# Two score additions moved from VectorE into TensorE's transposed bank, and two list rounds cut to one half of the candidates, in a sparse GATv2 + GCN kernel

## The chip, the cores and the metric

One core of one Trainium2 chip. The metric is the device time of one execution in microseconds. Fourteen runs of the kernel before gave a median of 3408.0 us, from 3378.63 to 3419.2 us.

## The reference

The input is `x` (3327 x 128) and a sparse symmetric matrix `adj` (3327 x 3327) with weights between 0.05 and 1 on its edges and on its diagonal; a row has 63 neighbours off the diagonal on average. Two layers follow each other. The first is a graph attention of four heads on `h = relu(layernorm(x))`:

```python
x1 = x @ w1; x2 = x @ w2
E = leaky_relu(x1[:, None, :] + x2[None, :, :], 0.01)
s = tanh((E @ a) / 8) * 8
s = exp(s) * A_shape
s = s / sum(s, axis=-1)
out = leaky_relu(s @ x @ Wlin.T, 0.01)
```

The heads are joined, multiplied by `w` and added to `x`. The second layer is `x + relu(A_norm @ (layernorm_relu(x) @ W.T + b))`, where `A_norm` is `adj + I`, scaled on both sides by the inverse square root of its row sums.

## The kernel before, in words

The kernel pads to 3328 rows: 26 blocks of 128 rows. It does not compute the attention scores of all pairs. For each row it finds the columns with an edge and gathers only those.

**Preparing a block** is the generator `prep(b, k)`. It transposes the block of `adj` (L365) and stores it (L370), multiplies the parts that the second layer can already use (L379), marks the edges as codes (L410), and takes the largest eight codes of each of 64 column segments (L422) into `cand`, two halves of 136 candidates. `select(r)` then runs 13 rounds: a MAX8 over the candidates (L453) and, in all but the last, a MATCH_REPLACE8 that strikes those eight out (L456). Rounds 0 to 3 alternate between the two halves (136 wide); the later ones run over both (272 wide). The first 64 entries of the list become the indices `idx` of 32 gathered tiles; up to 40 more go to a shared overflow of 256 places for each 64 rows. A row or half-block that does not fit raises a flag, and the kernel then computes everything again in a dense form. Near its end `prep` computes `x1b` and `x1n` and the table `pex`: the own-row score term of the block, `pmx` (L561), is multiplied by `modsel` on TensorE (L566) and copied out of PSUM by ScalarE (L568).

**The main loop** runs over (block, half of 64 rows, group of four tiles). Eight tiles are a window: four windows `w` and one overflow window (`ge`, three tiles) for each half, ten windows for each block, 260 in all. GpSimd gathers the tiles (L595) into one of four buffers `g`. `stage_z` transposes the gathered features into the PSUM bank pair `z` (L622, two bank pairs in turn, `hp` 0 and 1), and VectorE takes the maximum with `x1n` into `r` (L638), one of 1024 columns for each bank pair. `stage_r` multiplies `r` by the attention vector (L657) into `s` once for two groups.

`finish(k, hb, w)` is a generator too, one for each window. ScalarE copies `s` to `ssb` (L666); TensorE transposes that four times into a PSUM bank `tr` (L675); VectorE adds the gathered score term of the neighbour (L678) and then `pex`, or for the overflow window a term of `ex` (L681), into `sc`; ScalarE applies tanh (L686) and exp (L688); VectorE multiplies by the edge weights to `wt` (L697); TensorE sums the rows into `ag` (L706, or L724 for the overflow window), and `allow` gives the gather buffer free. `close` finishes a half block (L735 to L797).

**The order** is written by hand. `slot()` is called at fixed places in `stage_z` and after `stage_r`, 108 times for each block, and moves each open `close`, then each open `finish`, on by one `yield`, then `prep`, then the gathers. So the number of `yield`s between two steps sets how many slots lie between them in every engine's queue. The engines run their queues in order. The banks `tr` come from a pool of two that `prep`, `finish` and `close` share.

Of the kernel before, what the change touches and what calls it, by code (L numbers as in the profile page):

```python
# [9 lines left out]
F32 = mybir.dt.float32  # L10
AF = mybir.ActivationFunctionType
OP = mybir.AluOpType
# [3 lines left out]
P = 128  # L16
SLOPE = 0.01
CAP = 8.0
# [44 lines left out]
OVT = 3  # L63
# [168 lines left out]
def _sparse_layers(tc, nc, x, adj, w1, w2, a, wlin, w, gw, gb, gb_sb, gwT, x_sb, dinv, flag, ident, out):  # L232
# [13 lines left out]
    NP, D = x.shape  # L246
    H = w1.shape[0]
# [5 lines left out]
    WT = 8  # L253
    NW = NT // WT
    LATE = 1

    with ExitStack() as l0:
# [19 lines left out]
        modsel = res.tile([P, P], F32, name="modsel")  # L277
# [8 lines left out]
        pb = l0.enter_context(tc.tile_pool(name="pb", bufs=2))  # L286
# [41 lines left out]
        def bank():  # L328
            return ps_tr.tile([P, 4, P], F32, name="tr").rearrange("p a b -> p (a b)")
# [23 lines left out]
        def prep(b, k):  # L353
# [41 lines left out]
            SOME = 8 + 4 * 32  # L395
            cand = pb.tile([P, 2, SOME + 4 * 32], F32, name="cand", bufs=1)
# [51 lines left out]
            flat = cand[:, :, :SOME]  # L448

            def select(r):  # L450
                top = lists[:, 8 * r:8 * r + 8]
                of = cand[:, r % 2, :SOME] if r < 4 else flat
                nc.vector.max(top, of)  # L453
                yield
                if 8 * r + 8 < 2 * SLOTS + EXTRA:
                    nc.vector.match_replace(out=of, in_to_replace=top, in_values=of, imm_value=0.0)  # L456
                yield

            for r in range(SLOTS // 4):
                yield from select(r)  # L460
# [7 lines left out]
            pm = bank()  # L468
# [8 lines left out]
            for r in range(SLOTS // 4, SLOTS // 4 + EXTRA // 8):  # L477
                yield from select(r)
# [17 lines left out]
            pm = bank()  # L496
# [22 lines left out]
            pm = bank()  # L519
            ex_ps = pm[:, :2 * OVT * 46].rearrange("p (t c) -> p t c", c=46)  # L520
            for c in range(2):
                for t in range(FOUND):
                    nc.tensor.matmul(ex_ps[:, OVT * c + t, :], oi[:, (FOUND * c + t) * P:(FOUND * c + t + 1) * P], ext[:, :46],
                                     start=True, stop=True)
# [25 lines left out]
            pm = bank()  # L550
            nc.tensor.matmul(pm, hTb, w1_sb.rearrange("p h d -> p (h d)"), start=True, stop=True)
            x1b = pb.tile([P, H * D], F32, name="x1b")
            nc.scalar.copy(x1b, pm)
            yield
            pm = bank()
            for h in range(H):
                nc.tensor.matmul(pm[:, h * P:(h + 1) * P], w1_sb[:, h, :], hTb, start=True, stop=True)
            x1n = pb.tile([P, H, P], F32, name="x1n")
            nc.scalar.activation(x1n, pm[:, :H * P].rearrange("p (h i) -> p h i", h=H), AF.Copy, scale=-1.0)
            pmx = pb.tile([P, 16, H], F32, name="pmx", bufs=1)  # L560
            nc.vector.tensor_tensor(pmx, tmask[:, :, None].to_broadcast([P, 16, H]),  # L561
                                    p_all[:, b, None, :H].to_broadcast([P, 16, H]), OP.mult)
            yield
            yield
            pm = bank()
            nc.tensor.matmul(pm[:, :16 * H], modsel, pmx.rearrange("p t h -> p (t h)"), start=True, stop=True)  # L566
            pex = pb.tile([P, 16, H], F32, name="pex")
            nc.scalar.copy(pex, pm[:, :16 * H].rearrange("p (t h) -> p t h", h=H))  # L568
            k.x1b, k.x1n, k.pex = x1b, x1n, pex
            yield  # L570

        def rows_in():
# [88 lines left out]
        def finish(k, hb, w):  # L661
            g, s = k.g.pop((hb, w)), k.s
            f0 = k.f0[hb]
            nt, nk, nm = (WT, 4, 2) if w < NW else (OVT, OVT, 1)
            ssb = ph.tile([P, BANK], F32, name="ssb", bufs=1)
            nc.scalar.copy(ssb[:, :nk * P], s[:, :nk * P])  # L666
            if w < NW:
                wq = pb.tile([P, WT, 8], F32, name="wq")
                diag = bass.AP(g.tensor, g.offset + BODY * hb, [list(g.ap[0]), [WIDE + 8, 8], [1, 8]])
                nc.vector.tensor_tensor(wq, diag, qmask[:, None, :].to_broadcast([P, WT, 8]), OP.mult)  # L670
            yield
            yield
            pt = ps_tr.tile([P, 4, P], F32, name="tr")
            for q in range(nk):
                nc.tensor.transpose(pt[:, q, :], ssb[:, q * P:(q + 1) * P], ident)  # L675
            yield
            sc = pb.tile([P, WT, H], F32, name="sc")
            nc.vector.tensor_tensor(sc[:, :nt].rearrange("p (m k) h -> p m k h", m=nm),  # L678
                                    pt.rearrange("p k (h m) -> p m k h", m=32)[:, :nm, :nk],
                                    g[:, :, f0 + D:f0 + D + H].rearrange("p (m k) h -> p m k h", m=nm), OP.add)  # L680
            nc.vector.tensor_add(sc[:, :nt], sc[:, :nt], k.pex[:, 8 * hb:8 * hb + 8] if w < NW else  # L681
                                 k.ex[:, OVT * hb:OVT * hb + OVT, 42:42 + H])
            yield
            yield
            th = pb.tile([P, WT, H], F32, name="th")
            nc.scalar.activation(th[:, :nt], sc[:, :nt], AF.Tanh, scale=1.0 / CAP)  # L686
            pe = pb.tile([P, WT, H], F32, name="pe")
            nc.scalar.activation(pe[:, :nt], th[:, :nt], AF.Exp, scale=CAP)  # L688
            yield
            yield  # L690

            if w == 0:
                k.ag = ps_a.tile([P, 2, 256], F32, name="ag")
            ag = k.ag
            if w < NW:
                wt = pv.tile([P, WT, H, 8], F32, name="wt", bufs=2)
                nc.vector.tensor_tensor(wt, pe[:, :, :, None].to_broadcast([P, WT, H, 8]),  # L697
                                        wq[:, :, None, :].to_broadcast([P, WT, H, 8]), OP.mult)
                yield
                yield  # L700
                yield
                yield
                yield
                for t in range(WT):
                    u, cg = t // 4, t % 4
                    nc.tensor.matmul(ag[32 * cg:32 * cg + 32, u, :WORK], wt[:, t].rearrange("p h q -> p (h q)"),  # L706
                                     g[:, t, f0:f0 + WORK], start=(w == 0 and t < 4), stop=False, skip_group_check=True)
                allow("g")
                return
            am = pb.tile([P, OVT, HALF], F32, name="am", bufs=1)  # L710
            wo = pv.tile([P, OVT, 8, H, 8], F32, name="wo")
            for t in range(OVT):
                nc.vector.scalar_tensor_tensor(am[:, t, :], code[:, :HALF], k.ex[:, OVT * hb + t, 41:42], g[:, t, BODY * hb:BODY * hb + HALF],
                                               op0=OP.is_equal, op1=OP.mult)
                nc.vector.tensor_tensor(wo[:, t], pe[:, t, None, :, None].to_broadcast([P, 8, H, 8]),
                                        am[:, t].rearrange("p (g q) -> p g q", q=8)[:, :, None, :].to_broadcast([P, 8, H, 8]), OP.mult)
                yield
            yield
            yield
            yield  # L720
            yield
            for t in range(OVT):
                for u in range(2):
                    nc.tensor.matmul(ag[:, u, :WORK], wo[:, t, 4 * u:4 * u + 4].rearrange("p g h q -> p (g h q)"),  # L724
                                     g[:, t, f0:f0 + WORK], start=False, stop=(t == OVT - 1), skip_group_check=True)
            allow("ge")
            tails.append(close(k, hb))
# [75 lines left out]
        for b in range(NB):  # L803
            k = Blk()
# [6 lines left out]
        SLOTP = 6 * 2 * NG  # L811
        AHEAD = 0.5
        preps = [prep(b, blks[b]) for b in range(NB)]
        queue = deque()
        done = [0] * NB
# [29 lines left out]
        def allow(kind):  # L845
            state[kind] += 1
# [345 lines left out]
        with tc.manual_schedule():  # L1192
# [5 lines left out]
            def scores(i):  # L1198
                if 0 <= i < n:
                    b, hb, m = groups[i]  # L1200
                    stage_r(blks[b], hb, m, rs.pop(i))
                    if m % 2 or m == NG - 1:
                        ends.append(finish(blks[b], hb, m // 2))
                    slot()

            for i in range(-1, n + 1):
                if i + 1 < n:
                    slot()
                if 0 <= i < n:
                    b, hb, m = groups[i]  # L1210
# [153 lines left out]
```

## Time and profile before

| | before |
|---|---|
| median of 14 runs | 3408.0 us |
| profiled execution, its own time | 3427.39 us |
| span in its trace | 3425.7 us |
| mean granted TensorE clock | 0.883 |
| TensorE busy | 2644.0 us (77%) |
| VectorE busy | 2102.3 us (61%) |
| GpSimd busy | 1713.6 us (50%) |
| ScalarE busy | 683.1 us (20%) |
| DMA | 241 GB/s on average |

The profiled execution is 0.6% slower than the median of the runs. Busy times of engines overlap, so they do not add up to the span. In the groups of instructions a row names a line, an engine, an operation, output and inputs, the count, the total and mean time, and what the engine had waited for. A TensorE record is one pass: a transposing product of 128 columns is one record, a plain 32-bit product two.

### The profile page before, as it was taken

The page shows a single profiled execution, that of the slowest core. Times are in us where ns is not written, and L with a number is a line of the kernel's source. Part 1 is how long each engine was busy: PE and PEld are TensorE (multiplying, and loading weights), DVE is VectorE, ACT ScalarE, POOL GpSimd, SP SyncE. Part 2 cuts the span into 40 slices and gives each one's busy share as a digit, 9 for nine tenths or more (in the row PEclk, how much of TensorE's full clock was granted, in tenths as well). Part 3 has the DMA queues.
Part 4 walks back from the last instruction along what each step waited for, and adds up shares of the span by engine and source line. Part 5 has one row for each costly group of instructions (what it writes and reads, how often), then busy time and mean ns, then how long its engine had stood idle before and what let it go on. Part 6 is the DMA issues. An engine that isn't in the chain of part 4 may idle for free.

```text
span 3425.7 us, 52385 instructions
## 1 busy us (share of the span) xinstructions
PE 2644.0 (77%) x19410; PEld 1847.8 (54%) x19410; DVE 2102.3 (61%) x6426; ACT 683.1 (20%) x1703; POOL 1713.6 (50%) x1822
## 2 busy tenths in 40 slices
PE   6687777777777777777877777777877787777887
PEld 4455555545555555555655555555655555555553
DVE  6676566657656666665665665665665665665442
ACT  3122122212212212221221121221221221221110
POOL 3555555455555555545545545455555555445530
PEclk8799889898989989888888888888888888888999
DMA  9978678678768867867867867767776777777886
GB/s 324 316 259 263 211 247 267 204 244 279 226 221 261 261 213 246 263 206 244 259 197 246 267 199 243 253 215 233 249 231 215 247 232 226 232 224 216 261 272 184
DMA packets 417844, 826.94 MB, mean 241 GB/s; under 512 B 38435, under 2 KB 288815, under 8 KB 414255
## 3 DMA queue, kind: packets, MB, share of 16 engines
q0 software_dynamic: 141440, 619.41, 55.8%
q1 hardware_dynamic: 165343, 147.87, 13.9%
q10 hardware_dynamic: 110800, 56.25, 5.6%
q8 instruction: 156, 2.56, 0.3%
q14 instruction: 105, 0.86, 0.1%
HBM read 754.47 MB, written 113.22 MB: 253 GB/s over the span
## 4 chain that ended last, share of the span: by engine, by line
PE 53%; DVE 17%; another core or an unknown queue 11%; issue 10%; DMA 4%; ACT 1%; POOL 1%; ACTq 0%; SPq 0%; DVEq 0%; POOLq 0%
PE z L622 19%; PE s L657 11%; DVE r L638 9%; PE ag L706 5%; PE z L627 3%; PE tr L675 3%; DVE cand L422 3%; PE ag L724 2%; PE tr L379 2%; DVE codes L410 1%; POOL g L595 1%; PE tr L757 1%; DMA g<-AT_d 1%; PE z L988 1%
## 5 line engine op out<-in xcount | busy, mean ns | idle before, releaser
L595 POOL DMA_INDIRECT g<-table,idx x1664 | 1591.9, 957 | 1386.1 <-PE ag L706 813.3
L638 DVE TENSOR_TENSOR r<-z,x1n 128x1024 f32<-128x1024 f32 x832 | 1013.3, 1218 | 849.1 <-remote 318.9
L622 PE MATMUL z<-ident,g 128*128 128x128 f32 x6656 | 1050.8, 302 | 169.5 <-issue 111.8
L622 PEld LDWEIGHTS z<-ident,g 128*128 128x128 f32 x6656 | 856.3, 157 | 354.7 <-issue 232.4
L657 PE MATMUL s<-r,sel 128*2 128x512 f32 (+1 forms) x3744 | 549.8, 610 | 128.5 <-DVE r L638 94.5
L706 PE MATMUL ag<-g,wt 128*32 128x133 f32 x3328 | 237.8, 306 | 103.2 <-issue 102.2
L666 ACT COPY ssb<-s 128x512 f32<-128x512 f32 x260 | 146.9, 565 | 831.0 <-PE s L657 331.5
L657 PEld LDWEIGHTS s<-r,sel 128*2 128x2 f32 x3744 | 82.3, 84 | 402.9 <-issue 259.3
L706 PEld LDWEIGHTS ag<-g,wt 128*32 128x32 f32 x3328 | 135.6, 118 | 225.3 <-issue 217.4
L675 PE MATMUL tr<-ident,ssb 128*128 128x128 f32 x988 | 172.4, 300 | 92.3 <-issue 74.4
L422 DVE MAX8 cand<-codes 128x8 f32<-128x52 uint16 x1664 | 217.4, 205 | 0.0
L675 PEld LDWEIGHTS tr<-ident,ssb 128*128 128x128 f32 x988 | 129.8, 155 | 117.7 <-issue 89.9
L379 PE MATMUL tr<-at,x_sb 128*128 128x128 f32 x488 | 100.1, 363 | 115.4 <-ACT at L367 112.5
L595 POOL DMA_INDIRECT ge<-table,idxo x104 | 98.5, 947 | 177.4 <-PE ag L724 93.4
L367 ACT COPY at<-tr 128x512 f32<-128x512 f32 (+1 forms) x175 | 97.3, 556 | 417.7 <-remote 223.1
L686 ACT ACTIVATE th<-sc 128x32 f32<-128x32 f32 x260 | 58.4, 225 | 534.2 <-DVE sc L681 294.0
L379 PEld LDWEIGHTS tr<-at,x_sb 128*128 128x128 f32 x488 | 84.5, 258 | 143.9 <-ACT at L367 135.8
L365 PE MATMUL tr<-ident,adjb 128*128 128x128 f32 x676 | 124.6, 311 | 33.1 <-DMA adjb<-in_adj_dram 15.3
L633 DVE TENSOR_TENSOR r<-z,x1n 128x128 f32<-128x128 f32 x104 | 30.2, 290 | 190.5 <-PE z L627 135.3
L627 PE MATMUL z<-oi,x1b 128*128 128x256 f32 x416 | 133.5, 405 | 3.2 <-issue 3.2
L453 DVE MAX8 lists<-cand 128x8 f32<-128x272 f32 (+1 forms) x338 | 133.3, 394 | 2.2
L622 PE MATMUL z<-ident,ge 128*128 128x128 f32 x416 | 87.5, 287 | 43.7 <-issue 35.7
(199 smaller groups left out, 2627.9 us busy)
## 6 DMA issues: line engine op xcount, KB each, us to landing
adjb<-in_adj_dram SPq DMA_DIRECT2D x26, 1664.0 KB
table<-AT_d SPq DMA_DIRECT2D x26, 1664.0 KB
AT_d<-at ACTq DMA_DIRECT2D x150, 256.0 KB
g<-table,idx POOLq DMA_INDIRECT x1664
table<-img SPq DMA_DIRECT2D x12, 1296.0 KB
adjb<-AT_d SPq DMA_DIRECT2D x72, 128.0 KB
g<-AT_d SPq DMA_DIRECT2D x25, 256.0 KB
g<-AT_d ACTq DMA_DIRECT2D x25, 256.0 KB
```

Source lines behind the costliest of these rows:

```text
L365: nc.tensor.transpose(pt[:, q, :], adjb[:, (j0 + q) * P:(j0 + q + 1) * P], ident)
L379: nc.tensor.matmul(pq[:, :P], x_sb[:, j0 + q, :], at[:, q, :], start=(q == 0), stop=(q == js[-1]))
L422: nc.vector.max(cand[:, c, 8:].rearrange("p (r s) -> p r s", s=32)[:, :, sgm % 32], codes.rearrange("p a b -> p (a b)")[:, sgm % 32 * SEG: ...
L453: nc.vector.max(top, of)
L595: return nc.gpsimd.indirect_dma_start(out=g[:, t, lo:hi], out_offset=None, in_=tab, in_offset=bass.IndirectOffsetOnAxis(ap=at[:, t:t + 1], ...
L622: nc.tensor.matmul(z[:, i, q * P:(q + 1) * P], g[:, m % 2 * 4 + q, c0:c0 + D], ident, is_transpose=True, start=(q == 0 or m < 8), stop=(m ...
L627: nc.tensor.matmul(z[:, i, :n], k.x1b[:, h * D:(h + 1) * D], k.oi[:, hb * n:(hb + 1) * n], start=False, stop=True, skip_group_check=True)
L638: nc.vector.tensor_tensor(r.rearrange("p h (i s) -> p h i s", s=16), z.rearrange("p h (i s) -> p h i s", s=16), k.x1n[:, 2 * hp:2 * hp + 2 ...
L657: nc.tensor.matmul(k.s[32 * h:32 * h + 2, :n], sel[:, h, 31 - at:33 - at], r[h // 2][:, h % 2, :n], start=(at == 0), stop=(at == 1 or m == 8))
L666: nc.scalar.copy(ssb[:, :nk * P], s[:, :nk * P])
L675: nc.tensor.transpose(pt[:, q, :], ssb[:, q * P:(q + 1) * P], ident)
L706: nc.tensor.matmul(ag[32 * cg:32 * cg + 32, u, :WORK], wt[:, t].rearrange("p h q -> p (h q)"), g[:, t, f0:f0 + WORK], start=(w == 0 and t ...
```

## The change

`select` keeps to one half of the candidates for six rounds instead of four. The table `pex`, its product, its copy and two `yield`s go; `pmx` is kept in two buffers and handed to `finish`. In `finish` the two VectorE additions and two `yield`s go. In their place TensorE adds two products of 32 columns (12 in the overflow window) to the bank in which the transposed scores lie: the neighbour's term times the identity, and `pmx` times `modsel` (or the `ex` term times the identity). Tanh reads the bank.

```diff
@@ in prep: select @@
-                of = cand[:, r % 2, :SOME] if r < 4 else flat
+                of = cand[:, r % 2, :SOME] if r < 6 else flat
@@ at the end of prep @@
-            pmx = pb.tile([P, 16, H], F32, name="pmx", bufs=1)
+            pmx = pb.tile([P, 16, H], F32, name="pmx")
             nc.vector.tensor_tensor(pmx, tmask[:, :, None].to_broadcast([P, 16, H]),
                                     p_all[:, b, None, :H].to_broadcast([P, 16, H]), OP.mult)
-            yield
-            yield
-            pm = bank()
-            nc.tensor.matmul(pm[:, :16 * H], modsel, pmx.rearrange("p t h -> p (t h)"), start=True, stop=True)
-            pex = pb.tile([P, 16, H], F32, name="pex")
-            nc.scalar.copy(pex, pm[:, :16 * H].rearrange("p (t h) -> p t h", h=H))
-            k.x1b, k.x1n, k.pex = x1b, x1n, pex
+            k.x1b, k.x1n, k.pmx = x1b, x1n, pmx
             yield
@@ in finish @@
             yield
             pt = ps_tr.tile([P, 4, P], F32, name="tr")
             for q in range(nk):
-                nc.tensor.transpose(pt[:, q, :], ssb[:, q * P:(q + 1) * P], ident)
-            yield
-            sc = pb.tile([P, WT, H], F32, name="sc")
-            nc.vector.tensor_tensor(sc[:, :nt].rearrange("p (m k) h -> p m k h", m=nm),
-                                    pt.rearrange("p k (h m) -> p m k h", m=32)[:, :nm, :nk],
-                                    g[:, :, f0 + D:f0 + D + H].rearrange("p (m k) h -> p m k h", m=nm), OP.add)
-            nc.vector.tensor_add(sc[:, :nt], sc[:, :nt], k.pex[:, 8 * hb:8 * hb + 8] if w < NW else
-                                 k.ex[:, OVT * hb:OVT * hb + OVT, 42:42 + H])
-            yield
+                nc.tensor.matmul(pt[:, q, :], ssb[:, q * P:(q + 1) * P], ident, is_transpose=True, start=(q == 0), stop=False,
+                                 skip_group_check=True)
+            sc = pt.rearrange("p k (h m) -> p m k h", m=32)[:, :nm, :nk]
+            parts = [(ident, g[:, :nt, f0 + D:f0 + D + H])]
+            if w < NW:
+                parts.append((modsel, k.pmx[:, 8 * hb:8 * hb + 8]))
+            else:
+                parts.append((ident, k.ex[:, OVT * hb:OVT * hb + OVT, 42:42 + H]))
+            for at, (by, term) in enumerate(parts):
+                nc.tensor.matmul(sc, by, term.rearrange("p (m k) h -> p m k h", m=nm), start=False, stop=(at == 1), skip_group_check=True)
             yield
             th = pb.tile([P, WT, H], F32, name="th")
-            nc.scalar.activation(th[:, :nt], sc[:, :nt], AF.Tanh, scale=1.0 / CAP)
+            nc.scalar.activation(th[:, :nt].rearrange("p (m k) h -> p m k h", m=nm), sc, AF.Tanh, scale=1.0 / CAP)
```

## Prediction

> **What bounds the kernel now.** I read the page first, its busy times and its chain of work.
>
> ```profile
> PE 2644.0 (77%) x19410; PEld 1847.8 (54%) x19410; DVE 2102.3 (61%) x6426; ACT 683.1 (20%) x1703; POOL 1713.6 (50%) x1822
> ...
> PE 53%; DVE 17%; another core or an unknown queue 11%; issue 10%; DMA 4%; ACT 1%; POOL 1%; ACTq 0%; SPq 0%; DVEq 0%; POOLq 0%
> PE z L622 19%; PE s L657 11%; DVE r L638 9%; PE ag L706 5%; PE z L627 3%; PE tr L675 3%; DVE cand L422 3%; PE ag L724 2%; PE tr L379 2%; DVE codes L410 1%; POOL g L595 1%; PE tr L757 1%; DMA g<-AT_d 1%; PE z L988 1%
> ```
>
> TensorE is the busiest engine and holds over half of the chain, but it idles for 23% of the span. VectorE holds a sixth. The two take turns: TensorE fills a `z` bank pair, VectorE reduces it to `r`, TensorE needs `r`. So what moving work from one to the other is worth depends on who waits for whom where the work sits. Then the waits:
>
> ```profile
> ACT th L686 <- DVE sc L681: 294.0, 102, 9.6
> ...
> DVE r L638 <- PE z L622: 269.7, 153, 5.2
> ```
>
> The columns are microseconds in total, times, longest. ScalarE waits for the additions, and VectorE waits for TensorE before `r`. ScalarE is 20% busy, so its wait costs only where TensorE waits for ScalarE in turn.
>
> The place of the change is just behind the four transposes L675. The timeline of one window, VectorE's lines first and then TensorE's (start, length, operation; in brackets the idle time before it):
>
> ```profile
> 1794.32 1.22 DVE L638 TENSOR_TENSOR r<-z,x1n 128x1024 f32<-128x1024 f32 x1
> 1795.45 0.19 DVE L678 TENSOR_TENSOR sc<-tr,g 128x32 f32<-128x32 f32 x1
> 1795.67 0.20 DVE L681 TENSOR_TENSOR sc<-sc,pex 128x32 f32<-128x32 f32 x1
> 1795.79 1.01 DVE L422 MAX8 cand<-codes 128x8 f32<-128x52 uint16 x8
> 1796.83 0.29 DVE L425 MAX8 cand<-cand 128x8 f32<-128x128 f32 x1
> 1797.04 1.21 DVE L638 TENSOR_TENSOR r<-z,x1n 128x1024 f32<-128x1024 f32 x1
> ...
> 1798.30 1.09 PE L622 MATMUL z<-ident,g 128*128 128x128 f32 x8 [1.62 <-issue]
> ```
>
> VectorE runs without a gap from `r` through the additions and the list work to the next `r`; TensorE has stood still for 1.62 us when that `r` ends at 1798.25. Here VectorE is the bound. In other windows it is the other way round, as this line shows: VectorE idles 2.56 us until TensorE has filled the bank.
>
> ```profile
> 1376.40 1.23 DVE L638 TENSOR_TENSOR r<-z,x1n 128x1024 f32<-128x1024 f32 x1 [2.56 <-PE z L627]
> ```
>
> I counted in the trace, for every window, whether the two products `r` that follow the additions on VectorE started at once behind other VectorE work or after more than 0.1 us of idling. Both at once: 103 windows. Both waited: 71. The first at once, the second waited: 63. The reverse: 21. (Two have no such pair.) It repeats by the place of a window in its block: the windows in which the code scan and the list rounds run are VectorE's, those in which `close`, `oi`, `x1b` and the overflow window run are TensorE's. Between the transposes and the next scores L657 TensorE's idle time has a median of 2.0 us in the 103, of 0.0 in the 71, of 0.2 in the 63 and of 2.8 in the 21.
>
> **The change, part by part**, against the profiled execution's 3427.4 us.
>
> *TensorE gains two plain 32-column products for each window*, four records with a 128-column weight each. Nothing in the trace has that shape, so its price comes from the nearest plain ones:
>
> ```profile
> 1754.81 0.43 PE L566 MATMUL tr<-pmx,modsel 128*128 128x64 f32 x2
> 1755.08 0.39 PE L622 MATMUL z<-ident,ge 128*128 128x128 f32 x2
> ```
>
> From the start of the two 64-column records to the next start it is 0.27 us at full clock. Start to start, the 16-column records of L470 and the 46-column ones of L523 and L525 have a median of 0.111 us at full and of 0.213 us at half clock; a 128-column transposing record takes 0.109. So up to 128 columns the width hardly matters. The mean granted clock of 0.883 means half clock for 23% of the time: 0.77 x 0.111 + 0.23 x 0.213 = 0.135 us a record, 0.54 us a window, 140 us in 260 windows if all of it lay on the path. Bounds: 0.44 us (all full clock) and 0.85 us (all half).
>
> The Trainium skill ("TensorE: Matmul & The Clock Gate", section "Back-to-back issue gap") gives matmuls of 1 to 64 columns a floor of about 25 ns instead. The 111 ns of L470 contradict it for a stream that loads new weights each time. By the page the sum below would be an estimate of some 65 us less, which is a gain.
>
> *TensorE loses* 26 products L566, two records each: 26 x 0.27 = 7 us, in the overflow-window part of a block, where TensorE is the bound. ScalarE's 26 copies L568 (0.22 us each) go too; ScalarE idles there: nothing.
>
> *VectorE loses the additions and part of four list operations a block:*
>
> ```profile
> L678 DVE TENSOR_TENSOR sc<-tr,g 128x32 f32<-128x32 f32 x208 | 38.7, 186 | 57.1 <-remote 31.1 <-PE tr L675 13.9 <-PE ag L724 2.9
> L681 DVE TENSOR_TENSOR sc<-sc,pex 128x32 f32<-128x32 f32 x208 | 40.0, 192 | 7.2
> ...
> L453 DVE MAX8 lists<-cand 128x8 f32<-128x272 f32 x234 | 102.7, 439 | 2.2
> L453 DVE MAX8 lists<-cand 128x8 f32<-128x136 f32 x104 | 30.6, 294 | 0.0
> L456 DVE MATCH_REPLACE8 cand<-lists,cand 128x272 f32<-128x272 f32 x208 | 88.6, 426 | 0.0
> L456 DVE MATCH_REPLACE8 cand<-lists,cand 128x136 f32<-128x136 f32 x104 | 29.5, 284 | 0.0
> ```
>
> With the 52 overflow windows (8.7 and 8.9 us) the additions are 96.3 us, 0.37 a window, 0.40 with the gap between them. The list rounds 4 and 5 give 2 x 26 x (439 - 294 + 426 - 284) ns = 14.9 us.
>
> *What of this is on the path.* In the 103 windows of VectorE the bound shrinks by 0.40 us, as long as TensorE's idle time takes up 0.54 + 0.40. Window by window, the larger of (0.54 minus its idle time) and -0.40 sums to -34 us. In the 71 nothing hides the products: +38 us. In the 63 the second `r` comes later by the same: +34. In the 21 the idle time hides all but 2 us. Together +40. Minus 7 for L566. Of the list rounds' 14.9 us I take two thirds, 10 us, because they sit mostly in VectorE's windows (184 of the 476 products that start at once do so behind a list operation); ends 0 and 15. **Sum: +23 us, 3450 us for the profiled execution, 0.7%.**
>
> *Waits and moves, costed at nothing.* The new products wait for nothing new: `z` has waited for the same gathers already, `pmx` is a block old, the weights are constants. Tanh now waits for TensorE, not VectorE; behind it in ScalarE's queue stand `ssb`, `at` and `agn`, all of which depend on later TensorE work. It reads a bank instead of SBUF: L568, from a bank, takes 0.22 us, exp from SBUF 0.23. The bank `tr` is now released by tanh instead of by the first addition; TensorE's waits for that addition sum to 14 us, so I keep -15 to +15. Two `yield`s fewer put `wt`, `ag` and `allow` two slots earlier, some 2.3 us (a block is about 122 us, 108 slots). The sums `ag` now stand before the scores instead of behind them. GpSimd waits 813 us for `ag`, but its gathers are issued 20 us or more before their use in 95% of the windows, so that buys nothing. If that cover were gone it would be a gain of up to 2 us in a window. DMAs are the same.
>
> **Rivals.**
>
> 1. *TensorE is the bound nearly everywhere.* The chain has L675 for 3% of the span, 103 us; its 988 records at 0.135 us are 133, so 77% of it is on the path, and work right behind it would be too: 0.77 x 140 - 7 = +101 us; the additions hold under 1% there. For it: VectorE idles 39% of the span, and waits for TensorE. Against: the "issue" steps of the chain, such as the 1.62 us above, hide waits for `r`. It gives 3528, or 3508 on the median's scale. With all 140 it would be 3560.
> 2. *VectorE and ScalarE are the bound, and it gets faster.* Additions go from every window in which one of the two products started at once (187 x 0.40 = 75 us), all list work (15) and L566 (7) pay, and only the 71 windows cost (38): -59 us, 3368, or 3350 on the median's scale. It decides if TensorE's idle time behind the transposes in the 63 mixed windows is over 0.54 us; their median is 0.2, but their mean is 1.4 us. Against it stands that in those windows VectorE itself waits for `z`.
> 3. *It doesn't do what it says.* Six rounds on one half take zeros where a half has fewer than 24 edges, and push real ones into the overflow. Counted from the inputs, 75 main places stay empty and the fullest half-block needs 241 of 256 overflow places (240 before), so the dense path isn't taken; if it were, the time would be a multiple.
>
> **Numbers.** The profiled execution lies 0.6% above the median of 3408.0; the forecast on that scale is 3408 x 1.0067 = 3431 us. Its own range, from the price's bounds, the bank and the lists, is 3405 to 3475. Chances: forecast 0.46, rival 1 0.25, rival 2 0.28, rival 3 0.01. The range reaches to the values of both rivals: 3352 to 3507. About 0.3%, 10 us, is what a measurement here can tell from no change. The forecast's 0.46 splits into 0.33 slower, 0.10 the same and 0.03 faster; rival 1 is slower, rival 2 faster but for 0.02.
>
> **What would show it.** Right: the products of 32 columns at 0.11 us a record at full clock; VectorE's busy time down by about 110 us, TensorE's up by some 130; TensorE's idle time before `z` smaller in the windows with list work, VectorE's wait before `r` larger in those of the overflow window. Wrong: a price a record far from 0.11; L675 and its products nearly always on the chain (rival 1); VectorE's share of the chain fallen with TensorE's idle time larger than what was added (rival 2); a wait of TensorE for tanh to free the bank.

## The result and the profile after

The changed kernel takes 3768.6 us (median of 13 runs, 3751.0 to 3785.6) against 3409.2 (62 runs): a ratio of 1.106, 95% interval 1.104 to 1.108. It is 10.6% slower, far outside the range of 3352 to 3507. The profiled execution has a span of 3777.2 us, at a mean granted clock of 0.832 (0.883 before).

The busy times and the chain of the changed kernel's page, in the order of the lines shown for before:

```profile
PE 2826.0 (75%) x20398; PEld 1987.9 (53%) x20398; DVE 2018.7 (53%) x5906; ACT 668.2 (18%) x1677; POOL 1700.5 (45%) x1822
...
PE 61%; another core or an unknown queue 13%; issue 10%; DVE 8%; ACT 4%; DMA 3%; POOL 0%; ACTq 0%; SPq 0%; DVEq 0%
PE z L616 22%; PE s L651 12%; PE ag L701 5%; DVE r L632 4%; PE tr L669 3%; PE z L621 3%; PE ag L719 2%; PE tr L678 2%; PE tr L379 2%; PE tr L365 2%; ACT ssb L660 1%; PE tr L551 1%; PE tr L470 1%; PE z L983 1%
```

TensorE's busy time is 182 us longer, but the span is 351 us longer, and every engine's share has fallen: TensorE stands still for 951 us, 782 before. (In the changed kernel L616 is `z`, L632 `r`, L651 the scores, L660 `ssb`, L669 the transposes, L678 the new products, L681 tanh, L692 `wt`, L701 the sums `ag`.) The list of waits says where: those of TensorE and VectorE that are new or grown (in the kernel before TensorE never waited for tanh ahead of the fourth line's work, a transpose of `close`, and VectorE's waits ahead of `wt` came to 4.0 us; the columns are us in total, times, longest). First the two of them that the kernel before has, then those of the changed kernel:

```profile
PE z L622 <- DVE r L638: 61.0, 105, 2.6
...
PE tr L675 <- ACT ssb L666: 17.8, 15, 4.5
```

```profile
PE z L616 <- DVE r L632: 265.9, 101, 6.1
...
PE tr L669 <- ACT ssb L660: 202.8, 65, 4.6
...
DVE wt L692 <- issue: 153.1, 56, 4.3
...
PE tr L779 <- ACT th L681: 104.7, 23, 5.7
...
DVE wt L692 <- ACT pe L683: 91.6, 42, 5.5
```

Every engine waits for another. The timeline of the changed kernel shows how (start, length, engine, operation; in brackets the idle time before it):

```profile
1773.99 0.39 PE L678 MATMUL tr<-pmx,modsel 128*128 128x32 f32 x2
...
1774.47 1.07 PE L616 MATMUL z<-ident,g 128*128 128x128 f32 x8
1774.60 1.23 DVE L632 TENSOR_TENSOR r<-z,x1n 128x1024 f32<-128x1024 f32 x1 [0.24 <-issue]
...
1774.76 0.39 ACT L775 ACTIVATE agn<-xn,st 128x128 f32<-128x128 f32 x1
1775.05 0.19 ACT L775 ACTIVATION_READ_ACCUMULATOR agn<-xn,st 128x1 f32 x1
...
1780.38 0.20 ACT L681 ACTIVATE th<-tr 128x32 f32<-128x32 f32 x1 [5.15 <-remote]
1780.43 0.16 DVE L499 TENSOR_TENSOR lists<-hoff,tr 128x1 f32<-128x1 f32 x1 [4.60 <-remote]
1780.61 0.23 ACT L683 ACTIVATE pe<-th 128x32 f32<-128x32 f32 x1
```

From 1775.83 to 1780.38 no instruction is in progress on TensorE, VectorE or ScalarE. GpSimd's gathers run on (left out). By TensorE's records, whose ends are modelled, the products L678 that tanh reads were done at 1774.38; tanh starts 6.0 us after that. So TensorE stood still although its records say that it was done. I added up such silent stretches over 0.5 us in the records of the three engines: 280 us in the trace of before, 500 in that of the changed kernel. The granted clock fits: half clock for 801 us of before (23%) and for 1269 us of the changed kernel (34%). The two overlap with other waits, so they are marks of the loss and no sum. They are used below to compare kernels.

### The profile page after: what moved, and what is told of

It is laid out like the page before. It is cut to its first block, busy times and chain, and to the rows that moved or that the text cites. A ratio compares the mean times of both kernels' runs of the same rounds, so it can differ in the third digit from the quotient of the medians.

```text
span 3777.2 us, 53741 instructions
## 1 busy us (share of the span) xinstructions
PE 2826.0 (75%) x20398; PEld 1987.9 (53%) x20398; DVE 2018.7 (53%) x5906; ACT 668.2 (18%) x1677; POOL 1700.5 (45%) x1822
## 4 chain that ended last, share of the span: by engine, by line
PE 61%; another core or an unknown queue 13%; issue 10%; DVE 8%; ACT 4%; DMA 3%; POOL 0%; ACTq 0%; SPq 0%; DVEq 0%
PE z L616 22%; PE s L651 12%; PE ag L701 5%; DVE r L632 4%; PE tr L669 3%; PE z L621 3%; PE ag L719 2%; PE tr L678 2%; PE tr L379 2%; PE tr L365 2%; ACT ssb L660 1%; PE tr L551 1%; PE tr L470 1%; PE z L983 1%
## 5 line engine op out<-in xcount | busy, mean ns | idle before, releaser
L632 DVE TENSOR_TENSOR r<-z,x1n 128x1024 f32<-128x1024 f32 x832 | 1012.5, 1218 | 695.3 <-remote 385.5
L616 PE MATMUL z<-ident,g 128*128 128x128 f32 x6656 | 1144.5, 319 | 298.9 <-issue 157.4
L616 PEld LDWEIGHTS z<-ident,g 128*128 128x128 f32 x6656 | 938.3, 169 | 526.5 <-issue 357.9
L651 PE MATMUL s<-r,sel 128*2 128x512 f32 (+1 forms) x3744 | 509.1, 609 | 26.5 <-issue 20.8
L669 PE MATMUL tr<-ident,ssb 128*128 128x128 f32 x988 | 171.6, 298 | 239.8 <-ACT ssb L660 202.8
L660 ACT COPY ssb<-s 128x512 f32<-128x512 f32 x260 | 146.4, 563 | 1007.6 <-PE s L651 478.2
L669 PEld LDWEIGHTS tr<-ident,ssb 128*128 128x128 f32 x988 | 121.4, 150 | 269.8 <-ACT ssb L660 219.3
L651 PEld LDWEIGHTS s<-r,sel 128*2 128x2 f32 x3744 | 79.5, 85 | 289.3 <-issue 273.8
L692 DVE TENSOR_TENSOR wt<-pe,wq 128x256 f32<-128x256 f32 x208 | 87.8, 422 | 264.7 <-issue 153.1
L616 PE MATMUL z<-ident,ge 128*128 128x128 f32 x416 | 102.2, 334 | 137.7 <-DVE r L632 128.0
L681 ACT ACTIVATE th<-tr 128x32 f32<-128x32 f32 x260 | 50.4, 194 | 801.6 <-remote 362.4
L701 PE MATMUL ag<-g,wt 128*32 128x133 f32 x3328 | 191.4, 366 | 0.0
L616 PEld LDWEIGHTS z<-ident,ge 128*128 128x128 f32 x416 | 53.9, 161 | 212.3 <-DVE r L632 135.6
L701 PEld LDWEIGHTS ag<-g,wt 128*32 128x32 f32 x3328 | 104.1, 137 | 72.0 <-issue 64.6
L629 ACT ACTIVATE r<-z 128x512 f32<-128x512 f32 x104 | 62.1, 598 | 398.7 <-DVE r L627 307.4
```

Source lines behind the costliest of these rows:

```text
L616: nc.tensor.matmul(z[:, i, q * P:(q + 1) * P], g[:, m % 2 * 4 + q, c0:c0 + D], ident, is_transpose=True, start=(q == 0 or m < 8), stop=(m ...
L632: nc.vector.tensor_tensor(r.rearrange("p h (i s) -> p h i s", s=16), z.rearrange("p h (i s) -> p h i s", s=16), k.x1n[:, 2 * hp:2 * hp + 2 ...
L651: nc.tensor.matmul(k.s[32 * h:32 * h + 2, :n], sel[:, h, 31 - at:33 - at], r[h // 2][:, h % 2, :n], start=(at == 0), stop=(at == 1 or m == 8))
L669: nc.tensor.matmul(pt[:, q, :], ssb[:, q * P:(q + 1) * P], ident, is_transpose=True, start=(q == 0), stop=False, skip_group_check=True)
```

## Experiments

Times go with a ratio to the kernel before on the same chip in the same hour, since the chips differ: by the chip numbers on record the kernel before takes 3403 us on one, 3294 and later 3282 us on a second, 2502 on a third and 2501 on a fourth. Where two ratios come from different chips, a difference of a point or less between them tells little.

### Which part of the change costs it

**Two yields taken out of the kernel before**, nothing else (additions on VectorE, `pex` as it was):

```diff
                                  k.ex[:, OVT * hb:OVT * hb + OVT, 42:42 + H])
-            yield
-            yield
             yield
             th = pb.tile(...)
```

> The kernel before, with its additions on VectorE, but without the two yields between the additions and tanh. Theory 1 (the moves cost most of the 360 us: tanh, wt and ag stand two slots earlier in their engines' queues, and VectorE at wt and ScalarE at tanh stand still with other work behind them): 3600 to 3750 us, with VectorE idle before wt for over 200 us (4 us before). Theory 2 (TensorE's own added work costs it, some 140 us and more as the clock falls): 3380 to 3440 us. Theory 3 (the bank that tanh holds costs it): 3380 to 3440 us too, since the additions still free the bank's use from tanh.

3667.0 us, ratio 1.076 (1.073 to 1.079). The moves alone (tanh, exp, `wt`, the sums with `allow` behind them, and `close`) cost 7.6%. But VectorE's idle time before `wt` is 27 us, not over 200: the place was wrong in theory 1. TensorE waits 194 us for `ssb` instead, as in the changed kernel.

**TensorE's work alone**: the kernel before and two products of a zero tile into the bank.

```diff
+            for at in range(2):
+                nc.tensor.matmul(to, ident, nothing[...], start=False, stop=(at == 1))
             yield
             sc = pb.tile(...)
```

> The kernel before with two 32-column products of a zero tile added to the bank behind the transposes of each window; the additions stay on VectorE and every yield stays. It has TensorE's added work and nothing else of the change. Theory 1 (the moves): 3430 to 3550 us, the price of the products alone, between the +40 us that my count by windows gives and all 140 us. Theory 2 (TensorE's work): 3650 us or more.

3516.8 us, 1.033 (1.030 to 1.036): 111 us on the scale of 3409 (101 to 122). So the products alone are a third of the loss, within theory 1's bounds.

**The sum copied out of the bank**:

```diff
+            nc.vector.tensor_copy(held, sc)
+            yield
+            yield
             th = pb.tile(...)
-            nc.scalar.activation(th, sc, AF.Tanh, scale=1.0 / CAP)
+            nc.scalar.activation(th, held, AF.Tanh, scale=1.0 / CAP)
```

> The changed kernel, but VectorE copies the sum out of the bank one slot behind the products, and tanh reads the copy two slots later: the order of tanh, wt and ag and the early release of the bank are those of before, VectorE keeps one of its two small operations (0.19 us). Theories 1 and 3 (order, bank): 3380 to 3520 us. Theory 2 (TensorE's work): within 60 us of the changed kernel, 3700 to 3800 us.

3515.6 us, 1.033 (1.030 to 1.035), where theories 1 and 3 put their upper end: with the order of before, what is left is the price of the products. Theory 2 falls with both.

**`wt` and `ag` back in their slots**, tanh early and from the bank:

```diff
             nc.scalar.activation(pe[:, :nt], th[:, :nt], AF.Exp, scale=CAP)
+            yield
+            yield
             yield
             yield
```

> The changed kernel with two yields more between exp and wt: wt and ag stand in their slots of before, tanh and exp stay two slots early and tanh still reads the bank. If VectorE's standing at wt is the main loss (265 us of idle time before wt in the changed kernel, 4 before): 3450 to 3580 us. If tanh's place and the bank it holds are (TensorE waits 105 us for tanh before close's transposes, ssb is late behind tanh): 3680 us or more.

3474.5 us, 1.018 (1.013 to 1.022). Of the 10.6%, two yields take back all but 1.8, tanh's early place and the bank notwithstanding. The bank, which copy_out_vector frees early at 0.19 us of VectorE a window, costs nothing that shows. But several things moved here, so next each by itself.

**`wt` alone back, `ag` early** (two yields more after exp, three ahead of `ag` instead of five), and **`ag` alone back, `wt` early** (seven yields ahead of `ag` instead of five):

> The changed kernel with wt two slots later on VectorE, as before, but the sums ag (and with them the end of the half-block and close) in the early slots of the changed kernel. Theory A (VectorE stands still at wt): about 3475 us, like the kernel with both later. Theory B (the place of ag on TensorE is the loss: two slots earlier they stand in the same slot as the transposes L669 of the next window and ahead of them, and close moves too): 3700 us or more.

> The changed kernel with only the sums ag (and the end of the half-block) two slots later; tanh, exp and wt stay early. Theory A (VectorE stands still at wt): 3700 us or more, with over 200 us idle before wt. Theory B (the place of ag): 3460 to 3500 us, with the idle time before wt gone although wt stands where it did.

With `ag` early 1.103 (1.097 to 1.109), with `ag` back 1.027 (1.023 to 1.030). Theory A falls, and what moves with the sums costs some 8 points, `wt`'s place about 1 (ahead of `wt` VectorE still idles 55 us with `ag` back, where B had expected none). Other than the expectations say, the end of the half-block does not move with the sums: the yields directly ahead of `ag` are those of the four plain windows alone. So with `wt` back the overflow window's sums and `close` stand where they stood before, and the loss is there; with `ag` back they stay early, and it is gone. They are no part of it. But `allow`, the permission for the next gathers, stands directly behind the sums and moves with them in both kernels. The waits of TensorE agree with theory B. The kernel with early sums:

```profile
PE tr L669 <- ACT ssb L660: 236.4, 76, 4.7
PE z L616 <- DVE r L632: 198.5, 104, 6.0
```

and the one with both back in place (which waits 73.6 us for `z`'s `r`):

```profile
PE tr L669 <- ACT ssb L660: 13.4, 5, 4.5
```

**Without the products**: the kernel weights_later, but the g and mask terms of the scores are left out (no additions anywhere).

> The changed kernel with wt and ag in their slots of before and without the new products: the g and mask terms of the scores are left out. It tells what the products cost when VectorE has no additions: 3474.5 (with the products) less this. By my count by windows, VectorE's relief, L566 and the list rounds alone are worth 34 + 7 + 10 us: 3350 us. If VectorE's relief is worth nothing (TensorE bound nearly everywhere): 3390 to 3400 us. The products then cost 124 or about 80 us; with VectorE's additions in place they cost 113.

3245.2 us beside 3294.4: 0.986 (0.982 to 0.989), 49 us less on the scale of 3409 (38 to 60). VectorE's relief, L566 and the lists are worth what I had put on them, 51 us. That the sum came out so near doesn't check its single terms. The difference to weights_later, on another chip, gives the products 3.2%, 109 us, much as with VectorE's additions in place.

**The lists alone** (`r < 6` in the kernel before):

> The kernel before with nothing but six list rounds over halves in place of four. Predicted: 10 us less, 3393 us, between 0 and 15. If TensorE hides VectorE's list work: 3400 to 3405 us.

0.998 (0.996 to 1.0005): no difference that can be told; 10 us lie within the interval, 15 do not.

### What the place of the sums does

A window has 12 slots. Counted from its own scores, its sums stood at slot 12, right behind the next window's scores, and stand at slot 10 after the change, ahead of them. Four kernels ask what counts: one yield fewer ahead of `ag` in the kernel before (slot 11, ahead of the scores); two yields more there (slot 14, ahead of the transposes); the changed kernel with transposes and all that follows two slots later, but the sums at 10; the changed kernel with `allow` alone two slots later. In the first three `allow` moves with the sums.

```diff
sums_before_scores        sums_before_transposes     transposes_later         allow_later
                                                     +  yield                 +  yield
-  yield                  +  yield                   +  yield                 +  yield
                          +  yield                      pt = ps_tr.tile(...)     allow("g")
   for t in range(WT):       for t in range(WT):     -  yield, yield
      matmul(ag, ...)           matmul(ag, ...)         for t ...: matmul(ag)
```

> The kernel before with one edit: one yield fewer before ag. The sums of a window then stand directly ahead of the next window's scores on TensorE instead of directly behind them; additions, products, tanh, wt stay. Theory B1 (between the scores and the transposes the sums cover ScalarE's copy ssb; without them TensorE stands still at the transposes): 3600 us or more on a chip where the kernel before takes 3403 (ratio 1.05 to 1.10), with some 200 us of idle time of TensorE before the transposes for ssb (18 before). Theory B2 (later gathers, or a loss that grows with each slot): ratio up to 1.04 for a single slot, and no such wait for ssb.

> The changed kernel with its sums ag in their early place, but transposes, products, tanh, exp and wt two slots later, so that more z products lie between the scores and the transposes. B1 (the cover of ssb was lost): ratio 1.02 to 1.04, the wait for ssb below 30 us, although the sums are still early. If it is the sums' place itself, whatever covers ssb: 1.09 to 1.11.

> The changed kernel with only the permission for the next gathers two slots later, where it was before; ag itself early. If earlier gathers collide with something: ratio near 1.03. B1: no difference from the changed kernel, 1.10 to 1.11.

> The kernel before with two yields more before ag: the sums stand directly ahead of the next window's transposes, behind the z products that follow the scores. B1: they still lie between scores and transposes, so nothing is lost: ratio 0.99 to 1.01, and if ssb's wait is what little is left (18 us), at most 0.5% is won. If the loss grows with the distance from the place of before: 1.04 or more.

They ran on the chip where the kernel before takes 2501.7 us, and everything came out otherwise: 0.996 (0.994 to 0.997), 1.016 (1.013 to 1.019), 1.015 (1.012 to 1.018) and 0.997 (0.995 to 0.998). Early sums cost nothing that shows here. The lines of granted clock (40 slices of the span, tenths of full speed) show what is different about this chip. First the changed kernel of the first result, then sums_before_scores on this chip:

```profile
PEclk8778888878888888887888888888888888887989
```

```profile
PEclk9799999999999999999999999999999999999989
```

Half clock lasts 97 us here and the silent stretches come to 25 us. So the loss goes with a TensorE that pauses and slows down, and none of the theories of order had that in it. The transfers differ too. The same two pages' lines of the DMA engines' busy share:

```profile
DMA  9877677667667767766766766766766766765776
```

```profile
DMA  9999999999999999999999999999999999999975
```

The DMA engines are busy 97% of the span here (70% in the changed kernel of the first result), so they may be a bound of their own on this chip. Three of the four, and the changed kernel itself, follow on a chip like the first (kernel before 3282.0 us):

> The changed kernel as it is, beside the others. If TensorE's pauses and half clock (not the order of instructions alone) make the loss: a ratio of 1.09 to 1.11 where the kernel before takes 3250 us or more, and 1.01 to 1.02 where it takes 2500 us. If the order alone made it: 1.08 or more on both.

> The kernel before with the sums ag one slot earlier, directly ahead of the next window's scores on TensorE. On a chip where the kernel before takes 3250 us or more. Theory C1 (what counts is whether the sums stand behind the scores, where the pauses fall into them while VectorE has work): ratio 1.05 to 1.10, no pause over 0.6 us inside the sums, and the half-clock share up by 5 points or more. Theory C2 (the loss grows with each slot): 1.02 to 1.05. Theory C3 (the loss needs the change's other parts): 0.99 to 1.01.

> The changed kernel with early sums, but transposes, products, tanh, exp and wt two slots later. On a chip where the kernel before takes 3250 us or more. Theory B1 (the sums only covered ScalarE's copy ssb; the z products of two more slots cover it as well): 1.02 to 1.04. Theory C1 (the place of the sums behind the scores counts, whatever covers ssb): 1.08 to 1.11.

> The kernel before with the sums ag two slots later, directly ahead of the transposes of the next window, behind eight z products that follow the scores. On a chip where the kernel before takes 3250 us or more. C1 as stated needs them directly behind the scores: ratio 1.02 or more. B1: 0.99 to 1.01.

| kernel | sums at slot | ratio there | ratio on the 2502 us chip | half clock there | silent, us | gaps over 0.6 us inside the sums |
|---|---|---|---|---|---|---|
| before (its trace) | 12 | 1 | 1 | 23% | 280 | 146 |
| weights_later | 12 | 1.018 | | 24% | 268 | 112 |
| sums_alone_later | 12 | 1.027 | | 19% | 257 | 108 |
| sums_before_transposes | 14 | 1.016 | 0.997 | 23% | 295 | 147 |
| sums_before_scores | 11 | 1.050 | 0.996 | 27% | 304 | 3 |
| yields_out | 10 | 1.076 | | 31% | 474 | 0 |
| transposes_later | 10 | 1.077 | 1.016 | 30% | 347 | 0 |
| weights_alone_later | 10 | 1.103 | | 30% | 416 | 1 |
| changed kernel (first result) | 10 | 1.106 | | 34% | 500 | 0 |
| changed kernel again | 10 | 1.121 | | 33% | 410 | 0 |

The last column is worked out from the starts of TensorE's records: gaps over 0.6 us between two records of the same sums, which wait for nothing between them. The timeline of the kernel before has such a place, TensorE only:

```profile
1177.77 0.39 PE L706 MATMUL ag<-g,wt 128*32 128x133 f32 x5
1178.33 0.27 PE L706 MATMUL ag<-g,wt 128*32 128x133 f32 x1 [0.17 <-issue]
1179.81 0.27 PE L706 MATMUL ag<-g,wt 128*32 128x133 f32 x1 [1.21 <-issue]
1180.54 0.29 PE L706 MATMUL ag<-g,wt 128*32 128x133 f32 x1 [0.46 <-issue]
1181.26 0.43 PE L706 MATMUL ag<-g,wt 128*32 128x133 f32 x4 [0.43 <-issue]
```

The sums of one window, whose sixteen records take 0.66 us elsewhere, stretch from 1177.7 to 1181.7. Starts lie 1.48, 0.73 and 0.72 us apart, and that is typical: of the 182 gaps over 0.3 us in these sums 75 are 0.7 to 0.8 us, and 19 are 1.4 to 1.5.

With the sums behind the scores TensorE's pauses fall into the sums, some 130 us in all in the kernel before. With the sums ahead there are none inside them, but there is more silence elsewhere, and the sums themselves run at half clock more often than not. The three numbers after "x3328:" in the rows of line L706 of before, and L701 of the changed kernel, are the shortest, middle and longest record, in ns:

```profile
L706 PE MATMUL ag<-g,wt x3328: 273/277/431, 120.2 to 3340.2; 128*32 128x133 f32 x196
```

```profile
L701 PE MATMUL ag<-g,wt x3328: 274/428/431, 114.7 to 3692.9; 128*32 128x133 f32 x196
```

By the records that follow one another in the same sums, 18% lie in half clock before, 56% after.

The silence has one more mark, read from the DMA packets of the traces in steps of 0.1 us: it falls into the times when transfers run. In the changed kernel the DMA engines are less than 20% busy for 24% of the span, and 0.2% of the silence lies there; in the kernel before it is 18% of the span and 0.6%. During the gaps over 0.6 us inside the sums of before they are 94% busy on average, never under 63%. Transfers alone don't make the pauses, since the 2502 us chip has them nearly all the time without silence. But it keeps a rival open: earlier sums permit earlier gathers, and so move the transfers against TensorE's work. `allow` was put back by itself only on the 2502 us chip, where early sums cost nothing that shows. On the chips that pause no run tells the sums' place from the permission's.

So on such a chip: the sums one slot earlier, with `allow` and nothing else of the change, cost 5.0% (C1's lower edge, C2's upper one; half clock is 4 points above the trace of before, which is from another chip; C1 asked for 5). TensorE's wait for `ssb` is there, at half of what B1 had put:

```profile
PE tr L675 <- ACT ssb L666: 101.9, 24, 5.7
```

Covering `ssb` in another way takes back some 3 to 4 points (1.077 against 1.103 with `wt` alone back and against 1.121 for the changed kernel, on one chip), no more. In transposes_later_2 the wait for `ssb` is nearly gone, but TensorE idles 84.6 us ahead of the same transposes without a wait that the profile shows, and 6 points over weights_later remain:

```profile
PE tr L671 <- issue: 84.6, 25, 4.9
...
PE tr L671 <- ACT ssb L660: 7.3, 5, 2.5
```

B1 tells a part of it. Slot 14 costs 1.6%, between B1 and C1. C3 falls.

### Does the pause hang on the data?

Both kernels with w1 and w2 set to zero once the score vectors were made:

```diff
+                nc.vector.memset(w2_sb, 0.0)
+                nc.vector.memset(w1_sb, 0.0)
```

> The kernel before with the projection weights w1 and w2 set to zero once the score vectors are made: the projected features are left out, so z, x1b, x1n, r and the scores are zeros, while every instruction, transfer and wait stays; the features that ag sums are the real ones. Theory C (TensorE's pauses and half clock hang on how much its arithmetic works, so on the data): 3 to 25% less than the kernel before, with fewer pauses inside the sums and a smaller half-clock share. If they hang on the order and times of instructions alone: within 1% of it. (On a chip that takes 2500 us anyway: no difference, and nothing is told.)

> The changed kernel with the same zeros. Theory C: its time against before_zeros is 1.01 to 1.04, since the place of the sums costs nothing without pauses, and what stays is the products. If the order of the instructions makes the loss by itself: 1.10 to 1.12 against before_zeros.

These two fell on a chip where the kernel before takes 2501.4 us: 1.001 (0.999 to 1.002) and 1.018 (1.016 to 1.021). There zeros change nothing, and the changed kernel costs 1.7% over the one before with the same zeros, as weights_later does (1.8%) on a chip that pauses. Whether the data matters where TensorE pauses stays open.

No version that computes the full scores beats the kernel before where TensorE pauses: the two edits of `yield`s that win 0.4 and 0.3% on the 2502 us chip lose 5.0 and 1.6% on the others, and the six list rounds make no difference.

## Why the prediction was wrong

**The step that failed is "Waits and moves, costed at nothing"**, and in it this place: two yields fewer put `wt`, `ag` and `allow` two slots earlier, "the sums `ag` now stand before the scores instead of behind them", "so that buys nothing". It saw the move and asked only what it might win for the gathers. The move costs about 300 us: 1.106 against 1.018 of 3409. Of that `wt`'s place on VectorE is about 1 point and the rest, some 270 us (1.106 against 1.027), is the sums with `allow` behind them; the bank has no share that shows. What I didn't ask is what TensorE has to do between the scores and the transposes, while `ssb` is on its way. The runs show that the sums were part of that work (slot 12 against 11 and 10), that `ssb`'s cover is some 3 to 4 points of the loss, and that the loss appears only on chips where TensorE pauses and is granted half clock for 18% of the span or more. Why early sums lengthen the pauses stays open, and so does the share of `allow`: the prediction costed it at nothing because the gathers come 20 us ahead of their use, and no run on such a chip moves it alone.

**The products' price** was too high, their cover overrated. The second record of the first product starts 0.031 us behind the first, the steps after it are 0.112 each (every record has a weight load of its own, and these loads lie 0.110 to 0.112 apart throughout): 0.366 us a window at full clock, 0.712 at half, about 0.40 in the mix of weights_later, 104 us in all. I had 0.54 and 140. But I let TensorE's idle time hide nearly half of it and took 74 us; zero_products measures 111 (101 to 122). So the whole price is on the path and nothing hides it. Rival 1's 108 us (77% of 140) come near by luck: a price too high and a share too low. The groups of the changed kernel, by shape:

```profile
L678 PE MATMUL tr<-pmx,modsel 128*128 128x32 f32 x416 | 83.4, 283 | 0.0
...
L678 PE MATMUL tr<-g,ident 128*128 128x32 f32 x416 | 65.5, 240 | 0.0
```

The idle time of 2.0 us behind the transposes in 103 windows, read as VectorE's bound, hid nothing that shows; on a TensorE that pauses, "issue" can be its own pause. This last is argued, not shown.

The Trainium skill ("TensorE: Matmul & The Clock Gate", "Back-to-back issue gap") has a floor of about 25 ns between products of 1 to 64 columns. Three steps in four here are 112 ns instead, at the pace of the weight loads. The same section says that in a stream of weight loads and products both set the spacing, which the 112 ns fit; so the prediction's word that 111 ns contradict the page goes too far.

**VectorE's relief, L566 and the lists** were right as a sum: 51 us expected, 49 (38 to 60) measured. The lists may have a smaller part in it than I thought (5 us, from a gain of 13 to a loss of 2). The sum without the moves would have been 104 or 111 less 49, some 55 to 62 us; weights_later measures 60 (1.018). The forecast of 23 was too low by this, and that would have stayed in the range.

**What would show it**: VectorE's rows fell by 111 us as forecast (its busy time, which counts overlaps once, by 84), the products have their 0.11 us but for one record, TensorE's busy time rose by 182 instead of 130, since more of it ran at half clock. The sign of a bank that is held for tanh appeared (L779, 104.7 us) and misled: in weights_later, where tanh reads the bank as early, it is gone. Rival 2's sign appeared too, in a kernel that got slower: VectorE's share of the chain fell from 17 to 8%, and TensorE's idle time grew by 169 us.

## What to carry to other kernels

A step that is moved in a hand-written order has to be costed by what it leaves bare where it stood, and not only by what it meets in its new place: here eight short products between a result and its reader were the cover of a copy, and the loss is larger than that cover. Before a `yield` or a wait is taken out for tidiness, list on each engine what stands between producer and consumer before and after; here two yields alone are 7.6 of the 10.6%. And compare on one chip, with its clock beside the time: the same edit was −0.4% on one and +5.0% on another.

## What was unexpected in the hardware

The same kernel takes 2501 and 2502 us on two chips and 3282 to 3409 on others. On the fast ones its granted clock is 0.98, and in the trace of sums_before_scores three engines are silent together for 25 us; in the trace of the kernel before the clock is 0.883 and 280 us are silent, and rounds_only, which takes the same time, has 0.896 and 235 us on another. The page of the fast chip (sums_before_scores) has TensorE at 90%:

```profile
PE 2229.9 (90%) x19410; PEld 1586.3 (64%) x19410; DVE 2062.2 (83%) x6426; ACT 681.4 (27%) x1703; POOL 1729.1 (70%) x1822
```

TensorE there is not only granted more clock; the gaps of 0.72 us and its multiples inside a stream of products that waits for nothing are not there at all (none in 208 windows, against 146). Nine in ten of such gaps come at full granted clock (141 of 156, counting also those with another instruction in between), so the mean clock does not show them: by its ratio alone (0.883 to 0.98) the kernel would be 11% slower, and it is 36%. What makes TensorE pause was not found. The fetch of instructions does not fit: 14 of the 185 silent stretches of before have one of the 156 fetches within 1 us, and fetches at random times would give some 30.

The Trainium skill ("TensorE: Matmul & The Clock Gate", "What's actually happening") says that the clock is gated to half after an idle window of 3.4 us. The changes of the granted clock do lie 3.41 us or multiples of it apart here, and in the changed kernel half of the drops come within 1.0 us of the end of a silent stretch over 0.8 us. So the pauses may bring the half clock with them; no run here takes the pauses away alone to show it.
